# First batch of a fused four-layer block: small operations in another order, trace sums in two banks, weight splits moved

## The chip, the cores and the metric

The kernel runs on one core of a Trainium2 chip. The metric is device time in microseconds (us), the median of several executions. One further execution is taken with the hardware profiler, and the profile's times are counted from the start of its span.

## What is computed

For 16 batches of 256 tokens with 256 features, four residual layers follow each other. The first two, cut to what matters here:

```python
# layer 0: gated multi-time-scale traces (16 time constants, d = 0..15)
ctx   = ema(x, tau_ctx)                                   # scan over the tokens
gated = x * sigmoid([x, ctx] @ Wg.T + bg)
mod   = 0.5 + sigmoid(gelu(x @ Wn1.T + bn1) @ Wn2.T + bn2)     # one value per token and d
temporal = sum_d softmax(blend)[d] * ema(gated * mod[d], tau[d])
soma  = gelu(x @ Wsoma.T + bsoma)
out   = (soma * sigmoid(temporal @ Wtemp.T + btemp)) @ Wout.T
x = x + layernorm(out) * gamma + beta
# layer 1: masked softmax pooling
s = tanh(x @ W1 + b1) @ v
x = x + (softmax(mask(s)) @ x) / count
# layer 2: 8 experts + 1 shared, silu(x@Wg)*(x@Wu)@Wd, mixed by gates
# layer 3: gelu(x@W1+b1)@W2, and an expert part chosen per batch
```

Layers 2 and 3 hold nearly all of the arithmetic.

## The kernel before

**Number format.** Large products run in fp32r as three products of high and low parts. A "split" of an operand is two instructions: the high part is a rounding copy on ScalarE (`rnd("a", ...)`, line 88), the low part is operand minus high part (`low`, line 95), on VectorE (`"v"`) or GpSimd (`"g"`). `mm3` (lines 101 to 103) issues the three products. The first batch's own layers 0 and 1 use plain fp32 products on unsplit operands, so they wait for no split; all later batches need split small weights. These lie side by side in `wh` and `wl`: N1 (256 columns), G (1024, in two halves of 512), SO, TE, OU (512 each), W1 (256). Their unsplit forms are in `small_a` (N1, G, SO, W1) and `small_b` (TE, OU), filled by loads issued by SyncE's queue at the start.

**Stages.** Batch 0 goes through `first_traces` and `first_pooled` by itself. Only then can the expert loop of layer 2 start (first on batch 0 alone, for five of nine experts). Layers 0 and 1 of the later batches (`traces`, `pooled`) are cut into steps by `yield` and dealt out between the units of the expert loop. Batch 1's `traces` begins inside batch 0's `first_pooled`: of the 13 steps after the first 13, steps 16, 20 and 24 are batch 1's (x_1 and its ctx; c, ph, hg, hs; pm, md), and the other ten are batch 0's: 14 pt and tanh, 15 the product with soma, 17 po, statistics and rs, 18 the normalized x1, 19 transposes and x1T, 21 pa and tanh, 22 and 23 the softmax, 25 transposes and q, 26 pp, the addition into acc and the split of it.

**The first batch's traces.** After ph, hg and the gate products pg, `md` gives `mod`'s small rows, and `ms` is their split form. For each d a pair of selecting products spreads two rows over the partitions (`pb`), ScalarE scales them to `mod` (two pieces, line 529, two buffers), GpSimd (VectorE for d=0) multiplies by the gate (`bt`, line 532), VectorE scans (`tr`, two scans, line 535) and TensorE adds the scans up through an identity product (`tacc`, line 538, one 128x512 product in one PSUM bank). At d=5 the soma products and their two Gelus follow (lines 543 to 547). At the end `tacc` is evicted in two halves, one on ScalarE, one on VectorE (`evict`, lines 470 to 475), and pt reads the result.

**Order.** The framework gives each engine a fixed order. It takes it from a timing model: of the instructions that are ready there, the one that stands first in the program. `tc.issue_after(i)` puts the instructions traced inside the block behind `i` on `i`'s engine, and does nothing on other engines. `last_of` holds the latest of some kinds: `"ca"` a rounding copy or eviction on ScalarE, `"cv"` a low part or eviction on VectorE, `"a"` a mod piece, `"g"` a bt, `"tr"` a scan. A split with no such block may be put as early as its operand is there.

**Expert weights.** `load_chunk` loads one chunk (384 KB) into one of two `raw` buffers and splits it into one of ten ring buffers. `prefetch(2, 0)` brings chunks 0 and 1 (low parts on GpSimd) behind the traces; chunks 2 to 5 (low parts on VectorE) are asked for one by one at steps 19, 21, 23 and 25, and four more after step 26.

Of the kernel before, what the change touches and what calls it, by code (L numbers as in the profile page):

```python
# [17 lines left out]
S = 256  # L18
P = 128
# [25 lines left out]
def fused_kernel(  # L45
# [90 lines left out]
    def split_small(c0, n, e):  # L136
        rnd("a", wh[:, c0 : c0 + n], small(c0, n))
        low(e, wl[:, c0 : c0 + n], small(c0, n), wh[:, c0 : c0 + n])
# [117 lines left out]
    held = {}  # L256

    rest = {1: (O_SO, 512), 6: (O_TE, 512), 9: (O_OU, 512), 12: (O_W1, 256)}

    def traces(b):  # L260

        xr = xin_tiles.pop(b)
        xh, xl = hl(f"x_{b}", "hA")
        rnd("a", xh, xr)
        low("g", xl, xr, xh)
# [53 lines left out]
        for d in range(ND):  # L319
            if d % 2 == 0:  # L320
                mod = l0.tile([P, 2, S], F32, tag="mod", name=f"mod{b}_{d}", bufs=2)
                nc.sync.dma_start(mod, mdd[0, d : d + 2].partition_broadcast(P))
            bt = ft("bt", f"bt{b}_{d}", 3)
            tr = tacc if d == 0 else ft("tr", f"tr{b}_{d}", 3)
            with tc.issue_after(last_of[0].ins) if b == 1 and "h" not in last_of else nullcontext():
                for c in range(2):
                    V.scalar_tensor_tensor(
                        bt[:, c], ga[:, c], bl[:, c, d : d + 1], mod[:, d % 2], ALU.mult, ALU.mult
                    )
            for c in range(2):  # L330
                V.tensor_tensor_scan(  # L331
                    tr[:, c], decay[:, d : d + 1].to_broadcast([P, S]), bt[:, c], 0.0, ALU.mult, ALU.add
                )
            if d:
                G.tensor_tensor(tacc, tacc, tr, ALU.add)  # L335
            if b == 1 and d in rest:
                split_small(*rest[d], "g")
            if d == 5:
                soma()
            yield  # L340
# [136 lines left out]
    def first_traces():  # L477
# [14 lines left out]
        def gates_of(ks):  # L492
            for m in range(2):
                for k in ks:
                    i = xr[:, k] if k < 2 else cx[:, k - 2]
                    PE.matmul(pg[m], small(O_G + k * S + m * P, P), i, start=k == 0, stop=k == 3)

        gates_of((0, 1))
        yield
        pm = ps_l.tile([P, 512], F32, tag="ps", name="pm0")  # L500
        last_of["pm"] = PE.matmul(pm[:48, :S], vec[0:64, V_WN2 : V_WN2 + 48], hg[0:64], start=True, stop=True)
        md = l0.tile([48, S], F32, tag="md", name="md0")
        A.activation(md, pm[:48, :S], AF.Tanh, bias=hb[:48, V_BN2 : V_BN2 + 1], scale=0.5)
# [6 lines left out]
        with tc.issue_after(last_of["pm"].ins):  # L510
            gates_of((2, 3))
# [7 lines left out]
        tacc = ps_y.tile([P, 2, S], F32, tag="y0", name="ta0")  # L519
        for d in range(ND):  # L520
# [17 lines left out]
            PE.matmul(tacc, ident, tr, start=d == 0, stop=d == ND - 1)  # L538
            if d == 5:
# [6 lines left out]
                for m in range(2):  # L546
                    A.activation(sm[:, m], pso[:, m], AF.Gelu, bias=vec[:, V_BSO + m : V_BSO + m + 1])
# [3 lines left out]
        for c in range(2):  # L551
            evict(c, t[:, c], tacc[:, c])
# [6 lines left out]
    def first_pooled():  # L559
# [28 lines left out]
        G.tensor_tensor(rs, rs, mhalf, ALU.pow)  # L588
# [354 lines left out]
    while n_steps[0] < FIRST:  # L943
        next(steps)
        if n_steps[0] == 4:
            with tc.issue_after(last_of["cx"].ins):
                later_constants()
    with tc.issue_after(last_of["a"].ins), tc.issue_after(last_of["g"].ins), tc.issue_after(last_of["tr"].ins):
        for off, n in ((O_N1, 256), (O_G, 512), (O_G + 512, 512)):
            split_small(off, n, "g")  # L950
# [4 lines left out]
    while n_done[0] < 1:  # L955
        with tc.issue_after(last_of["ca"].ins), tc.issue_after(last_of["cv"].ins):
            next(steps)
            if n_steps[0] > FIRST + 5 and n < 6 and n_steps[0] % 2:
                prefetch(1, 0)
                n += 1  # L960
    with tc.issue_after(last_of["ca"].ins), tc.issue_after(last_of["cv"].ins):
# [157 lines left out]
```

## Time and profile before

| | |
|---|---|
| median of 3 runs | 2829.91 us (2829.66 to 2830.13) |
| profiled execution, time | 2829.02 us |
| profiled execution, span | 2827.0 us |
| granted TensorE clock, mean over the span | 0.996 |
| TensorE busy | 2774.3 us (98%) |
| VectorE, ScalarE, GpSimd busy | 1454.9, 1248.6, 1299.3 us |
| first expert product | at 60.40 us |

The span goes from the first to the last instruction; some 2 us of the time lie outside it. In lines in order of time the columns are start, duration (or, with a count, from the first's start to the last's end), engine, line of the program, operation, output and inputs by name, shape, count, and in brackets the idle time before it and what ended it. PEld is the weight load of TensorE, which overlaps its products.

### The profile page before, as it was taken

The numbers are of one execution on the slowest core, as the hardware profiler recorded it, in microseconds if no ns is written. First come the engines' busy times: TensorE is split into PE (matmuls) and PEld (weight loads), VectorE is DVE, ScalarE is ACT, GpSimd is POOL, SyncE is SP. The second block draws the span as 40 slices with busy tenths as digits, with TensorE's granted clock in tenths as the row PEclk, the third lists the DMA queues.
The fourth block names the chain that finished last, engine by engine and source line by source line (L and its number), as shares of the span: only waits on it lengthen the run. The fifth ranks groups of instructions, "written<-read, shape, count | busy, mean of one in ns | idle before, by whom it ended". The sixth has DMA issues, their size and how long they took to land.

```text
span 2827.0 us, 36929 instructions
## 1 busy us (share of the span) xinstructions
PE 2774.3 (98%) x13604; PEld 2331.4 (82%) x13604; DVE 1454.9 (51%) x2662; ACT 1248.6 (44%) x2062; POOL 1299.3 (46%) x986
## 2 busy tenths in 40 slices
PE   7889999999999999999999999999999999999999
PEld 4877898888888888888888888888888888888888
DVE  6988877865666363544545444444444542222222
ACT  5565565465444533435334443344433453233334
POOL 5755645544545353544534444444444443333333
PEclk9999999999999999999999999999999999999999
DMA  4453376396443533324433153331533242222453
GB/s 118 138 153 118 104 242 214 121 309 207 151 150 123 177 114 105 120 81 135 153 107 106 41 179 112 108 120 62 177 101 112 92 162 98 90 90 89 167 177 118
DMA packets 116998, 377.53 MB, mean 134 GB/s; under 512 B 12898, under 2 KB 31186, under 8 KB 116818
## 3 DMA queue, kind: packets, MB, share of 16 engines
q1 hardware_dynamic: 116386, 375.11, 40.1%
q8 instruction: 108, 1.77, 0.3%
q14 instruction: 72, 0.59, 0.1%
q10 hardware_dynamic: 432, 0.06, 0.0%
HBM read 310.91 MB, written 64.21 MB: 133 GB/s over the span
## 4 chain that ended last, share of the span: by engine, by line
PE 82%; DVE 7%; DMA 4%; ACT 3%; issue 2%; POOL 1%; SPq 0%; DVEq 0%; ACTq 0%; POOLq 0%
PE pg L102 8%; PE pg L103 8%; PE pg L101 8%; PE pu L103 8%; PE pu L102 8%; PE pu L101 8%; PE y L103 8%; PE y L102 8%; PE y L101 8%; DMA raw_e<-in_wexp_dram 4%; DVE w_e L95 2%; DVE tr L331 1%; ACT w_e L88 1%; PE z L101 1%; PE z L103 1%
## 5 line engine op out<-in xcount | busy, mean ns | idle before, releaser
L95 POOL TENSOR_TENSOR hh<-h,hh 128x512 fp32r<-128x512 f32 x640 | 847.7, 1325 | 1318.8 <-ACT hh L88 1298.2
L743 DVE TENSOR_TENSOR h<-h,pu 128x512 f32<-128x512 f32 x576 | 393.9, 684 | 907.4 <-PE pu L103 805.6
L88 ACT ACTIVATE hh<-h 128x512 fp32r<-128x512 f32 x640 | 403.5, 631 | 933.8 <-DVE h L743 911.6
L101 PE MATMUL pg<-x,w_e 128*128 128x512 f32 (+1 forms) x1232 | 466.0, 378 | 10.2 <-DVE h L743 6.4
L742 ACT ACTIVATE h<-pg 128x512 f32<-128x512 f32 x576 | 343.1, 596 | 299.1 <-PE pg L103 236.5
L101 PE MATMUL pu<-x,w_e 128*128 128x512 f32 (+1 forms) x1232 | 465.3, 378 | 6.9 <-ACT h L742 6.7
L103 PE MATMUL pg<-x,w_e 128*128 128x512 f32 (+1 forms) x1232 | 464.6, 377 | 1.5 <-DVE w_e L95 1.2
L102 PE MATMUL pg<-x,w_e 128*128 128x512 f32 (+1 forms) x1232 | 464.4, 377 | 1.1 <-POOL x L95 1.1
L102 PE MATMUL y<-hh,w_e 128*128 128x512 f32 (+1 forms) x1232 | 462.8, 376 | 2.2 <-POOL hh L95 2.2
L102 PE MATMUL pu<-x,w_e 128*128 128x512 f32 (+1 forms) x1232 | 463.5, 376 | 0.0
L103 PE MATMUL pu<-x,w_e 128*128 128x512 f32 (+1 forms) x1232 | 463.4, 376 | 0.0
L103 PE MATMUL y<-hh,w_e 128*128 128x512 f32 (+1 forms) x1232 | 462.7, 376 | 0.0
L101 PE MATMUL y<-hh,w_e 128*128 128x512 f32 (+1 forms) x1232 | 416.2, 377 | 2.8 <-ACT hh L88 1.6
L335 POOL TENSOR_TENSOR ta<-ta,tr 128x512 f32<-128x512 f32 x225 | 310.5, 1380 | 87.3 <-DVE tr L331 77.1
L331 DVE TENSOR_TENSOR_SCAN tr<-decay,bt 128x256 f32<-128x256 f32 x450 | 285.6, 671 | 0.0
L101 PEld LDWEIGHTS pg<-x,w_e 128*128 128x128 f32 x1232 | 232.3, 189 | 54.1 <-DVE h L743 8.9
L101 PEld LDWEIGHTS pu<-x,w_e 128*128 128x128 f32 x1232 | 232.5, 189 | 50.4 <-ACT h L742 9.5
L101 PEld LDWEIGHTS y<-hh,w_e 128*128 128x128 f32 x1232 | 231.5, 189 | 46.8 <-ACT hh L88 2.6
L102 PEld LDWEIGHTS y<-hh,w_e 128*128 128x128 f32 x1232 | 232.4, 189 | 44.6 <-POOL hh L95 2.9
L103 PEld LDWEIGHTS pg<-x,w_e 128*128 128x128 f32 x1232 | 232.4, 189 | 44.4 <-DVE w_e L95 2.0
L103 PEld LDWEIGHTS pu<-x,w_e 128*128 128x128 f32 x1232 | 232.5, 189 | 41.9
L103 PEld LDWEIGHTS y<-hh,w_e 128*128 128x128 f32 x1232 | 232.3, 189 | 41.8
(279 smaller groups left out, 3263.2 us busy)
## 6 DMA issues: line engine op xcount, KB each, us to landing
w_e<-keep_e SPq DMA_DIRECT2D x216, 768.0 KB, 4.2
raw_e<-in_wexp_dram SPq DMA_DIRECT2D x160, 384.0 KB, 3.7
keep_e<-w_e SPq DMA_DIRECT2D x72, 768.0 KB, 4.3
mod<-mdd SPq DMA_DIRECT2D x120, 256.0 KB, 3.6
w_f<-keep_f SPq DMA_DIRECT2D x56, 384.0 KB, 3.5
raw_c<-in_comb_dram SPq DMA_DIRECT2D x32, 260.0 KB, 2.7
xr<-in_xT_dram SPq DMA_DIRECT2D x16, 256.0 KB, 3.5
xt<-in_x_dram SPq DMA_DIRECT2D x16, 256.0 KB, 2.6
```

Source lines behind the costliest of these rows:

```text
L88: last_of["ca"] = A.activation(out_, in_, AF.Copy)
L95: i = (V if e == "v" else G).tensor_tensor(out_, in_, h.bitcast(F32), ALU.subtract)
L101: PE.matmul(o, wh, xh, start=start, stop=False, **kw)
L102: PE.matmul(o, wh, xl, start=False, stop=False, **kw)
L103: last_of["pe"] = PE.matmul(o, wl, xh, start=False, stop=stop, **kw)
L331: V.tensor_tensor_scan(tr[:, c], decay[:, d : d + 1].to_broadcast([P, S]), bt[:, c], 0.0, ALU.mult, ALU.add)
L335: G.tensor_tensor(tacc, tacc, tr, ALU.add)
L742: A.activation(h, ps_g, AF.Silu)
L743: last_of["h"] = V.tensor_tensor(h, h, ps_u, ALU.mult)
```

## The change

The soma Gelus move from d=5 to d=9 and d=11, each behind the latest mod piece. The gate products are issued as: first half (x part), pm behind it, second half (x part), then both ctx parts. The trace sum is kept in two banks, one per half, with two 256-wide products per d. Batch 1's x is split right behind the traces instead of in step 16. The splits of SO, TE, OU and W1, which stood in batch 1's trace loop, are taken apart: high parts behind md; low parts on VectorE, TE in step 21, the others in step 25. The high parts of N1 and G stay behind the traces, as does N1's low part; G's low parts go to GpSimd behind rs (step 17). The prefetch of steps 19 to 25 now stands in a block of its own that is entered after the step, so it is put behind the `ca` and `cv` of that step instead of those before it.

```diff
--- before.py
+++ after.py
@@ -133,8 +133,10 @@
     def load_small(c0, c1):
         nc.sync.dma_start(small(c0, c1 - c0), wsmall[:, c0:c1])
 
-    def split_small(c0, n, e):
-        rnd("a", wh[:, c0 : c0 + n], small(c0, n))
+    def high_small(c0, n):
+        A.activation(wh[:, c0 : c0 + n], small(c0, n), AF.Copy)
+
+    def low_small(c0, n, e):
         low(e, wl[:, c0 : c0 + n], small(c0, n), wh[:, c0 : c0 + n])
 
 
@@ -254,15 +256,20 @@
         return l0.tile([P, 2, S], F32, tag=tag, name=name, bufs=bufs)
 
     held = {}
-
-    rest = {1: (O_SO, 512), 6: (O_TE, 512), 9: (O_OU, 512), 12: (O_W1, 256)}
+    early_x = {}
+
+    def split_x(b):
+        xh, xl = hl(f"x_{b}", "hA")
+        rnd("a", xh, xin_tiles[b])
+        low("g", xl, xin_tiles[b], xh)
+        early_x[b] = xh, xl
 
     def traces(b):
 
+        if b not in early_x:
+            split_x(b)
+        xh, xl = early_x.pop(b)
         xr = xin_tiles.pop(b)
-        xh, xl = hl(f"x_{b}", "hA")
-        rnd("a", xh, xr)
-        low("g", xl, xr, xh)
         cx = ft("ta", f"ctx{b}")
         for c in range(2):
             V.tensor_tensor_scan(
@@ -333,8 +340,6 @@
                 )
             if d:
                 G.tensor_tensor(tacc, tacc, tr, ALU.add)
-            if b == 1 and d in rest:
-                split_small(*rest[d], "g")
             if d == 5:
                 soma()
             yield
@@ -489,18 +494,18 @@
         A.activation(hg, ph[:, :S], AF.Gelu, bias=vec[:, V_BN1 : V_BN1 + 1])
         pg = two("pg0")
 
-        def gates_of(ks):
-            for m in range(2):
-                for k in ks:
-                    i = xr[:, k] if k < 2 else cx[:, k - 2]
-                    PE.matmul(pg[m], small(O_G + k * S + m * P, P), i, start=k == 0, stop=k == 3)
-
-        gates_of((0, 1))
+        def gates_of(m, ks):
+            for k in ks:
+                i = xr[:, k] if k < 2 else cx[:, k - 2]
+                last_of["pg"] = PE.matmul(pg[m], small(O_G + k * S + m * P, P), i, start=k == 0, stop=k == 3)
+
+        gates_of(0, (0, 1))
         yield
         pm = ps_l.tile([P, 512], F32, tag="ps", name="pm0")
-        last_of["pm"] = PE.matmul(pm[:48, :S], vec[0:64, V_WN2 : V_WN2 + 48], hg[0:64], start=True, stop=True)
+        with tc.issue_after(last_of["pg"].ins):
+            last_of["pm"] = PE.matmul(pm[:48, :S], vec[0:64, V_WN2 : V_WN2 + 48], hg[0:64], start=True, stop=True)
         md = l0.tile([48, S], F32, tag="md", name="md0")
-        A.activation(md, pm[:48, :S], AF.Tanh, bias=hb[:48, V_BN2 : V_BN2 + 1], scale=0.5)
+        last_of["md"] = A.activation(md, pm[:48, :S], AF.Tanh, bias=hb[:48, V_BN2 : V_BN2 + 1], scale=0.5)
         V.tensor_scalar(md, md, 0.5, 1.0, ALU.mult, ALU.add)
         ms = l0.tile([48, S], F32R, tag="ths", name="ms0")
         rnd("v", ms, md)
@@ -508,7 +513,9 @@
         yield
         ga = ft("ga", "ga0")
         with tc.issue_after(last_of["pm"].ins):
-            gates_of((2, 3))
+            gates_of(1, (0, 1))
+            for m in range(2):
+                gates_of(m, (2, 3))
         for m in range(2):
             A.activation(ga[:, m], pg[m], AF.Tanh, bias=hb[:, V_BG + m : V_BG + m + 1], scale=0.5)
         for c in range(2):
@@ -516,7 +523,7 @@
         yield
         sm = ps_a.tile([P, 2, S], F32, tag="ga", name="sm0")
 
-        tacc = ps_y.tile([P, 2, S], F32, tag="y0", name="ta0")
+        tacc = [ps_y.tile([P, 512], F32, tag=f"y{c}", name=f"ta0{c}")[:, :S] for c in range(2)]
         for d in range(ND):
             if d % 2 == 0:
                 pb = ps_gu.tile([P, 2, S], F32, tag="gu", name=f"pb0_{d}")
@@ -535,7 +542,8 @@
                 last_of["tr"] = V.tensor_tensor_scan(
                     tr[:, c], decay[:, d : d + 1].to_broadcast([P, S]), bt[:, c], 0.0, ALU.mult, ALU.add
                 )
-            PE.matmul(tacc, ident, tr, start=d == 0, stop=d == ND - 1)
+            for c in range(2):
+                PE.matmul(tacc[c], ident, tr[:, c], start=d == 0, stop=d == ND - 1)
             if d == 5:
                 pso = ps_l.tile([P, 2, S], F32, tag="ps", name="pso0")
                 with tc.issue_after(last_of["pb"].ins):
@@ -543,13 +551,15 @@
                         for k in range(2):
                             w = small(O_SO + k * S + m * P, P)
                             PE.matmul(pso[:, m], w, xr[:, k], start=k == 0, stop=k == 1)
-                for m in range(2):
+            if d in (9, 11):
+                m = (d - 9) // 2
+                with tc.issue_after(last_of["a"].ins):
                     A.activation(sm[:, m], pso[:, m], AF.Gelu, bias=vec[:, V_BSO + m : V_BSO + m + 1])
             if d % 2:
                 yield
         t = ft("bt", "t0", 3)
         for c in range(2):
-            evict(c, t[:, c], tacc[:, c])
+            evict(c, t[:, c], tacc[c])
         xt = xt_tiles.pop(0)
         with tc.issue_after(last_of["g"].ins):
             last_of["g"] = G.tensor_tensor(xt, xt, bet.unsqueeze(1).to_broadcast([P, 2, S]), ALU.add)
@@ -585,7 +595,7 @@
             V.bn_stats(st[:, t], po[t])
             V.bn_aggr(mv[:, t], st[:, t])
         V.tensor_scalar(rs, mv[:, :, 1], 4e-5, None, ALU.add)
-        G.tensor_tensor(rs, rs, mhalf, ALU.pow)
+        last_of["rs"] = G.tensor_tensor(rs, rs, mhalf, ALU.pow)
         for t in range(2):
             V.scalar_tensor_tensor(po[t], po[t], mv[:, t, 0:1], gam, ALU.subtract, ALU.mult)
         yield
@@ -945,9 +955,18 @@
         if n_steps[0] == 4:
             with tc.issue_after(last_of["cx"].ins):
                 later_constants()
+
+
+    gates_w = ((O_G, 512), (O_G + 512, 512))
+    rest_w = ((O_SO, 512), (O_OU, 512), (O_W1, 256))
+    with tc.issue_after(last_of["md"].ins):
+        for off, n in ((O_TE, 512), *rest_w):
+            high_small(off, n)
     with tc.issue_after(last_of["a"].ins), tc.issue_after(last_of["g"].ins), tc.issue_after(last_of["tr"].ins):
-        for off, n in ((O_N1, 256), (O_G, 512), (O_G + 512, 512)):
-            split_small(off, n, "g")
+        split_x(1)
+        for off, n in ((O_N1, 256), *gates_w):
+            high_small(off, n)
+        low_small(O_N1, 256, "g")
         prefetch(2, 0)
 
 
@@ -955,9 +974,17 @@
     while n_done[0] < 1:
         with tc.issue_after(last_of["ca"].ins), tc.issue_after(last_of["cv"].ins):
             next(steps)
+        pool = last_of.get("rs", last_of["g"])
+        with tc.issue_after(last_of["ca"].ins), tc.issue_after(last_of["cv"].ins), tc.issue_after(pool.ins):
+            if n_steps[0] == 17:
+                for off, k in gates_w:
+                    low_small(off, k, "g")
             if n_steps[0] > FIRST + 5 and n < 6 and n_steps[0] % 2:
                 prefetch(1, 0)
                 n += 1
+
+            for off, k in {21: ((O_TE, 512),), 25: rest_w}.get(n_steps[0], ()):
+                low_small(off, k, "v")
     with tc.issue_after(last_of["ca"].ins), tc.issue_after(last_of["cv"].ins):
         coefs()
         prefetch(RING - n)
```

## The prediction

> **What bounds the kernel now.** I read the stretches of the run first, then the chain that ended last, then each engine's instructions in order of time for the first 62 us, because all that the change touches runs there.
>
> TensorE is busy 98% of the span. What it loses it loses at the front: busy time falls short by some 15 us before 60 us, and by some 27 us between 60 and 400 us, where the stretches show VectorE full and TensorE waiting for it.
>
> ```profile
> PE 2774.3 (98%) x13604; PEld 2331.4 (82%) x13604; DVE 1454.9 (51%) x2662; ACT 1248.6 (44%) x2062; POOL 1299.3 (46%) x986
> 90.00:100.00 10.00, 7.74 (x59) 7.06 (x58) 10.00 (x18) 2.80 (x4) 8.45 (x6) 1.00 0.42 131
> 300.00:400.00 100.00, 98.06 (x645) 88.70 (x644) 80.96 (x136) 61.92 (x105) 48.48 (x34) 1.00 0.50 160
> ```
>
> (In the stretches: length, then busy us of PE, PEld, DVE, ACT, POOL, granted clock.) The first expert matmul starts at 60.40. Until then the first batch is one chain, and all that starts behind it starts with it. So the question is by how much 60.40 moves, and whether the rest moves along.
>
> The chain's first part, by instructions in order of time:
>
> ```profile
> 11.74 0.42 ACT L88 ACTIVATE wh<-small_a 128x256 fp32r<-128x256 f32 x1 [0.81 <-DMA small_a<-in_wsmall_dram]
> 12.07 0.45 ACT L503 ACTIVATE md<-pm,hb 48x256 f32<-48x256 f32 x1
> 13.21 0.69 DVE L90 CAST ms<-md 48x256 fp32r<-48x256 f32 x1
> 14.94 2.50 ACT L529 ACTIVATE mod<-pb,bl 128x256 f32<-128x256 f32 x6 [1.70 <-PE pb L524]
> 20.53 15.98 POOL L532 TENSOR_TENSOR bt<-ga,mod 128x512 f32<-128x512 f32 x13 [1.46 <-ACT mod L529]
> 21.82 15.99 DVE L535 TENSOR_TENSOR_SCAN tr<-decay,bt 128x256 f32<-128x256 f32 x26 [1.45 <-POOL bt L532]
> 39.03 0.38 ACT L473 ACTIVATE t<-ta 128x256 f32<-128x256 f32 x1 [1.30 <-PE ta L538]
> 39.45 0.42 DVE L475 COPY t<-ta 128x256 f32<-128x256 f32 x1 [1.63 <-ACT t L473]
> ```
>
> See four things. A split of a later batch's weight, waiting for its load, stands ahead of md in ScalarE's queue. The trace loop then runs at 15.98/13 = 1.23 us per trace on GpSimd and as much (two scans) on VectorE. It stopped once, for 1.46, while mod stood behind the soma Gelu (18.76, ScalarE idle 1.33 for pso). At the end VectorE's eviction waits for ScalarE's, out of the same bank.
>
> The second part, near 48 us:
>
> ```profile
> 47.27 0.95 DVE L95 TENSOR_TENSOR w_e<-raw_e,w_e 128x768 fp32r<-128x768 f32 x1
> 48.53 0.36 ACT L473 ACTIVATE x1T<-ptr0g 128x256 f32<-128x256 f32 x1
> 49.30 0.42 DVE L475 COPY x1T<-ptr0u 128x256 f32<-128x256 f32 x1
> 59.47 0.42 DVE L645 TENSOR_TENSOR acc<-x1T,pp0g 128x256 f32<-128x256 f32 x1 [1.90 <-PE pp0g L643]
> 62.66 2.11 DVE L95 TENSOR_TENSOR w_e<-raw_e,w_e 128x768 fp32r<-128x768 f32 x1 [0.41 <-ACT w_e L88]
> ```
>
> The transposes end at 47.84, but ScalarE and VectorE take x1T only after a chunk's split and batch 1's c, hg, hs.
>
> **The change, part by part.** Times are those of the old trace; a gain moves all behind it.
>
> *Start.* The high parts of TE, SO, OU, W1 go behind md, their low parts leave GpSimd at 9 to 14 us, and pm is issued between the two halves of the gates. pm: 10.17 to 9.21 (end of the first gate pair); md: 12.07 to 9.75, done 10.2. VectorE's constants and md, ms ran stretched beside those GpSimd subtractions (the kind_i cast took 1.28, ms 0.69); without them ms is there at about 11.2 instead of 14.35. But ga does not come earlier: the same gate matmuls and pm still end at 12.73, the second tanh at 13.24. From there four mod pieces of 0.42 end at 14.92, and GpSimd's first bt starts at 14.95 instead of 16.59: **1.65**. What is late next is the gates. The four highs cost ScalarE 3x0.55+0.35 = 2.0 between md (10.2) and the first tanh (11.8, not the last): 0.4 over, hidden by the second tanh. If the order puts all of them behind the tanh, the loop starts 2.0 later and this part is -0.35; if pb slips in front of the gates it is 1.9. I take 1.65, as all four operands were there by 11.74.
>
> *Soma Gelu to traces 9 and 11.* The 1.46 goes. ScalarE has 0.39 free per trace (0.84 of 1.23); a Gelu of 0.46 exceeds it by 0.07, twice: **+1.3**. The last scan moves from 37.81 to 34.86. VectorE does not forbid it: 32 scans of 0.615 from 14.8 end at 34.5.
>
> *Two banks.* Two 256-wide products replace a 512-wide one of about 1.05 us; each pt product of 256 took about 0.43, so the loop's TensorE time is unchanged (sixteen more loads of ident hide beside it; if not, 0.2 a trace at most, under the 1.23). From the last scan to the last pt it took 41.46-37.81 = 3.65: sum, eviction, eviction, four pt. With c=0 summed and evicted during the last scan: 0.55 for the c=1 sum, 0.45 to evict, 1.0 for the last two pt, in all 2.05: a gain of 1.6. Against it, ScalarE's queue after the last mod (32.0) now holds x_1, N1, the two gates and two chunks, 3.6, so until 35.6, and the c=0 sum is there at 34.9: between 0 and 0.7 lost; I take 0.3. **+1.3**. Running sum 4.25.
>
> *GpSimd after the loop.* xt, x_1, N1, two chunks: 1.27+1.25+0.65+3.6 = 6.8 from 33.6 is 40.4; rs comes at 45.65-4.25 = 41.4. Before, it came 0.02 after GpSimd got free. Cost nothing, with 1 us of cover. The gates' low parts follow rs; their first reader is batch 1's gate product after 62 us.
>
> *Chunks of the prefetch.* In the old loop the waits of step and prefetch are taken together; in the new one the prefetch takes them after the step, so chunk 2 and then c, hg, hs stand behind x1T. x1T at 47.85 lets the second pa go 1.1 earlier. But the tanh th now has chunk 2, c, hg, hs ahead of it on ScalarE: 0.83+0.55+0.46+0.35 = 2.2 from 48.1, so 50.3 instead of 51.02. Chunk 3 (0.75) falls between th and the table load of 1.28: Exp at 52.8 instead of 53.27. No transfer is late by it: chunk 2's buffer is freed by GpSimd's chunk 0, which comes 4 us sooner; chunk 5's low part ends near 58 instead of 57.04, so chunk 7's load (about 3.1) lands at 61.1, before ScalarE takes it (61.9 now).
>
> *Low parts on VectorE.* TE (0.69 by the row of c at 48.13) lies in a wait of 2.09 at 50.7. SO, OU, W1 (0.69+0.69+0.42) come before the acc addition; with md 0.28 and chunk 5's 0.95 they are 3.03 from 56.4, so 59.45, and acc stood at 59.47. That eats the 0.5 won just before. Both parts together: **+0.2**, between -1.0 and +1.1. Here a rule speaks against the change. Chunk 2's low part took 0.95 with GpSimd idle, 2.11 at 62.66 with GpSimd on a chunk. The Trainium skill, "GPSIMD Engine Reference", 1. Specifications, says the two engines share SBUF interfaces and contend when a VectorE instruction has two SBUF inputs; each new low part has two. By the rule alone the four double, 2.5 more, and the gain would be 2.0. By the rows GpSimd is idle from 46.43 to 61.97 but for 1.59 at 50.24; the gates' low parts fill 2.5 us after rs, beside chunk 2 and c, not beside SO, OU, W1. TE may double, inside its 2.09. I go by the rows and keep the 2.5 for the range.
>
> *Behind 60 us.* Nothing is removed there: the splits written into batch 1's trace loop already ran at 8 to 14 us. VectorE's queue is the same and starts earlier, so the 27 us of waits shift whole. 0, between -2 and +2.
>
> Sum: 1.65+1.3+1.3+0.2 = 4.45. The profiled execution took 2829.02 for a span of 2827.0 (2.0 outside); the span becomes 2822.55, that time 2824.6. The median of the runs is 0.9 above the profiled one: 2829.91-4.45 = 2825.5.
>
> **Rivals.** 0.2% is 5.66 us, about what a measurement of this kernel can tell from no change.
>
> *A, the sum holds:* 2825.5, itself between 2823 and 2828. Chance 0.48; a third of that passes the bound at 2824.25.
>
> *B, the clock comes back too.* The second half of the chain runs cold:
>
> ```profile
> 46.00:48.00 2.00, 1.37 (x9) 0.74 (x7) 1.58 (x4) 1.97 (x5) 0.44 (x1) 1.00 0.45 172
> 58.00:60.00 2.00, 2.00 (x6) 1.29 (x4) 0.42 (x1) 0.07 (x1) 0.00 (x0) 0.50 0.86 329
> ```
>
> (the clock is the third figure from the end). The clock halves after TensorE was busy 0.48 of 2 us at 44. The Trainium skill, "TensorE: Matmul & The Clock Gate", Part 1, has a free-running window of about 3.4 us, whose load sets it. The gap before pa shrinks by 0.8, so the fall may come later. At full clock the chain's pa 0.6, psc 0.6, ppt 0.3 and three pp (0.86 to 0.43 each) 1.3 would give 2.8 more: 2822.7. For: the shorter gap. Against: ph of batch 1 leaves that gap, and pa to pp wait often. With other waits that may vanish, 0.27.
>
> *C, given back later.* The chain turns to DMA and VectorE at 64 us, and TensorE waits at 186 for batch 1's split. If that point is held by transfers instead of the chain, 60.40 moves and it does not: 2829.5. Against: its queue is VectorE's, 95% full. 0.13.
>
> *D, slower: low parts in front of acc.* Steps' low parts stand ahead of acc in VectorE's queue. Stretched as at 62.66 (2.2 times), 2.5 become 5.5; the gap is 1.9, so acc slips 3.6 and the gain falls to 0.85. The chunks' low parts behind slip as much, and each frees one of only two raw buffers: two rounds of 3.6 are 7.2 us of supply. Net 6.4 slower: 2836.3. It decides if the first expert matmul comes after 60.4. Against: GpSimd has nothing queued there. 0.12.
>
> **Numbers.** Faster by over 0.2%: 0.16 of A and B's 0.27, 0.43. Within: 0.32 of A and C, 0.45. Slower: 0.12. The likeliest is A. The range, 2821 to 2831.5, holds A, C and most of B, and leaves out D and B's far end.
>
> **What would show it.** In the new profile: bt's first on GpSimd near 15.0 and no stop of 1.4; the last scan near 34.9; VectorE's t not behind ScalarE's; pt over by 37.2; x1T straight after the transposes; SO, OU, W1 over before acc; first expert matmul near 56. A last scan after 36.5 makes the start wrong; 56 with an unmoved end is C; low parts of over 1 us ahead of acc are D; clock 1.0 from pa to pp is B.

## The result, and the profile after

| | before | after |
|---|---|---|
| median | 2829.59 us (22 runs) | 2833.6 us (22 runs, 2829.35 to 2839.56) |
| profiled execution, time; span | 2829.02; 2827.0 us | 2829.35; 2827.5 us |
| first expert product | 60.40 us | 56.92 us |

The ratio is 1.0014 [1.0009, 1.002]: slower by 4.0 us, where 4.45 less were forecast, and outside the range. The profiled execution is the fastest of the 22, so its trace shows less loss than the median has. Its front looks much as forecast. The chain's first part, instructions in order of time of the kernel after:

```profile
9.88 0.47 ACT L508 ACTIVATE md<-pm,hb 48x256 f32<-48x256 f32 x1 [1.42 <-PE pm L506]
10.70 0.29 DVE L90 CAST ms<-md 48x256 fp32r<-48x256 f32 x1
13.09 2.50 ACT L536 ACTIVATE mod<-pb,bl 128x256 f32<-128x256 f32 x6
14.74 18.48 POOL L539 TENSOR_TENSOR bt<-ga,mod 128x512 f32<-128x512 f32 x15 [13.35 <-ACT mod L536]
14.69 19.84 DVE L542 TENSOR_TENSOR_SCAN tr<-decay,bt 128x256 f32<-128x256 f32 x32
34.85 0.38 ACT L478 ACTIVATE t<-ta 128x256 f32<-128x256 f32 x1
35.31 0.42 DVE L480 COPY t<-ta 128x256 f32<-128x256 f32 x1 [0.79 <-PE ta L546]
```

md no longer stands behind a waiting split; GpSimd's 15 bt run in one piece from 14.74 (forecast 14.95); the last scan ends at 34.53 (forecast 34.86); VectorE's t waits for its own sum and not for ScalarE. The second part, with SyncE's queue and ScalarE behind it:

```profile
43.18 0.38 ACT L478 ACTIVATE x1T<-ptr0g 128x256 f32<-128x256 f32 x1 [5.40 <-PE ptr0g L611]
43.40 0.42 DVE L480 COPY x1T<-ptr0u 128x256 f32<-128x256 f32 x1 [0.69 <-PE ptr0u L611]
54.82 0.95 DVE L95 TENSOR_TENSOR w_e<-raw_e,w_e 128x768 fp32r<-128x768 f32 x1
55.99 0.42 DVE L655 TENSOR_TENSOR acc<-x1T,pp0g 128x256 f32<-128x256 f32 x1 [0.23 <-PE pp0g L653]
56.92 0.39 PE L101 MATMUL pg<-x,w_e 128*128 128x256 f32 x1 [0.17 <-ACT x L88]
56.22 0.80 SPq L329 DMA_DIRECT2D mod<-mdd  x2
57.13 6.79 SPq L682 DMA_DIRECT2D raw_e<-in_wexp_dram  x3
61.72 0.85 ACT L88 ACTIVATE w_e<-raw_e 128x768 fp32r<-128x768 f32 x1 [3.32 <-DMA raw_e<-in_wexp_dram]
```

x1T follows its transposes at once (but pa, which reads it, does not start at once: see below); the acc addition waits for its product and not for the low parts ahead of it; the first expert product is 3.48 earlier. But ScalarE now waits 3.32 for a chunk (chunk 7) that stands ahead of the table load for the first Silu. That Silu starts at 63.88, where it was 63.94. A new wait at the handover takes most of the front's gain, at first. The page's row for the engines and the four stretches shown of before:

```profile
PE 2775.1 (98%) x13636; PEld 2335.3 (83%) x13636; DVE 1455.0 (51%) x2666; ACT 1249.5 (44%) x2062; POOL 1294.1 (46%) x982
46.00:48.00 2.00, 1.44 (x5) 0.62 (x3) 1.97 (x2) 0.65 (x2) 1.02 (x1) 0.50 0.64 197
58.00:60.00 2.00, 2.00 (x19) 2.00 (x19) 0.68 (x4) 0.40 (x1) 1.52 (x1) 1.00 0.99 263
90.00:100.00 10.00, 7.86 (x52) 7.49 (x51) 10.00 (x20) 3.33 (x5) 7.39 (x6) 0.83 0.50 144
300.00:400.00 100.00, 97.94 (x648) 88.79 (x647) 81.38 (x136) 60.86 (x103) 47.37 (x34) 1.00 0.51 162
```

The clock still falls before pa (0.50 at 46). It is at 1.00 from 58 on, where expert products run now. TensorE has 32 more products and 32 more loads than before (13604 each). That pair of numbers turned out to matter most.

To see where the rest goes I matched the h addition (VectorE's `h<-h,pu`, one for each unit of the expert loop, numbered from 0) between two traces and took the difference. The lag against the first profile of before, in us, with the columns' names those of the runs below:

```
unit (at)      after  after_again  before_again  before_aa
1    (71)      -2.14     +0.40        -1.13        -0.46
31   (247)     -1.11     +2.76        -1.15        -0.19
84   (500)     -1.09     +3.75        -0.63        -0.91
88   (518)     -0.41     +4.23        -0.63        -0.91
94   (545)     -0.41     +4.23        -0.63        -0.91
100  (599)     +1.23     +5.17        -0.39        -0.93
end            +0.5      +5.9         -0.5         -0.9
```

Three losses: at the start (after_again, whose profiled execution is the slowest of its 13, never had the gain), between the first product and the second h, and in two steps at 500 to 518 and at 545 to 599, hundreds of microseconds behind anything that was edited.

### The profile page after: what moved, and what is told of

Its sections match the earlier page's. It is cut to its first block, busy times and chain, and to the rows that moved or that the text cites. A ratio compares the mean times of both kernels' runs of the same rounds, so it can differ in the third digit from the quotient of the medians.

```text
span 2827.5 us, 36992 instructions
## 1 busy us (share of the span) xinstructions
PE 2775.1 (98%) x13636; PEld 2335.3 (83%) x13636; DVE 1455.0 (51%) x2666; ACT 1249.5 (44%) x2062; POOL 1294.1 (46%) x982
## 3 DMA queue, kind: packets, MB, share of 16 engines
q8 instruction: 108, 1.77, 0.3%
## 4 chain that ended last, share of the span: by engine, by line
PE 82%; DVE 6%; DMA 5%; ACT 3%; issue 2%; POOL 1%; SPq 0%; DVEq 0%; ACTq 0%; POOLq 0%
PE pg L102 8%; PE pg L103 8%; PE pg L101 8%; PE pu L103 8%; PE pu L102 8%; PE pu L101 8%; PE y L101 8%; PE y L103 8%; PE y L102 8%; DMA raw_e<-in_wexp_dram 4%; DVE w_e L95 2%; ACT w_e L88 1%; DVE tr L338 1%; PE z L101 1%; PE z L102 1%
## 5 line engine op out<-in xcount | busy, mean ns | idle before, releaser
L101 PEld LDWEIGHTS pu<-x,w_e 128*128 128x128 f32 x1232 | 232.2, 189 | 51.5 <-ACT h L752 10.7
```

Source lines behind the costliest of these rows:

```text
L101: PE.matmul(o, wh, xh, start=start, stop=False, **kw)
```

## The experiments

Medians are of this kernel and of before on the same chip, each with its ratio and interval; 12 to 22 runs of a changed kernel, 22 to 65 of before. "Order" is each engine's fixed order.

### The handover at 60 us: SyncE's queue, and the prefetch's block

Three kernels on one chip: after unchanged; after with chunk 7's load ahead of batch 1's mod transfers (which wait for mdd); after with the prefetch back in the step's own block.

```diff
 # after_sp
+    with tc.issue_after(last_of["raw", 0, 7].ins) if b == 1 and d == 0 else nullcontext():
         nc.sync.dma_start(mod, mdd[0, d : d + 2].partition_broadcast(P))
...
-            nc.sync.dma_start(raw, wexp[key[2]])
+            last_of["raw", key[1], key[2]] = nc.sync.dma_start(raw, wexp[key[2]])
 # after_pf
         with tc.issue_after(last_of["ca"].ins), tc.issue_after(last_of["cv"].ins):
             next(steps)
+            if n_steps[0] > FIRST + 5 and n < 6 and n_steps[0] % 2:
+                prefetch(1, 0)
+                n += 1
```

> The changed kernel itself, timed and profiled once more. Its first profile has the first expert product 3.5 us earlier, a gain of 2.1 left from the second product of the loop on, and 0.5 us lost at the end, but its median is 4 us above before, so one trace doesn't show where most of the loss lies. Theory 1 (the loss is made at the transfers, between 230 and 800 us, and differs from run to run): front as in the first trace within 0.2 us, the lag to before then moves by several us between 400 and 800 us, at other places than in the first trace. Theory 2 (a fixed cost of the new order right behind the front): the same lag curve as in the first trace within 0.3 us, and the time near 2829.5. Ratio to before 1.001 to 1.002 by both.

> The changed kernel with one edit: batch 1's mod transfers are put behind chunk 7's load on SyncE's queue, as they stood before; the order of every engine is otherwise the same. In the changed kernel chunk 7's load goes out at 57.1 behind two mod transfers that wait for mdd, and ScalarE's first Silu stands behind chunk 7's high part. Theory 1a (this queue order eats 1.3 of the front's 3.5 us, and nothing more): first h 3.3 to 3.6 us earlier than before instead of 2.1, the median 1.3 below the changed kernel's. Theory 1b (the late chunk also sets the loss in the transfers behind it): median 4 to 6 us below the changed kernel's, at 2826 to 2828. Rival (the front's gain is lost at a later point whatever it was): lag at 500 us as in the changed kernel, median the same within 1 us.

> The changed kernel with one part undone: chunks 2 to 5 are prefetched inside the step's own block again, so their splits are put behind the step before, as before the change. Theory 1: chunk 7's load is in front of the mod transfers again, so the first h gains the 1.3; x1T waits for chunk 2 again (0.7 to 1.1 lost): lag at the first h about -2.5, and the median 1 us or less from the changed kernel's. Theory 3 (the new place of the prefetch is what spoils the transfers of the loop): median 4 us or more below the changed kernel's.

Measured: after_again 2831.95 against 2828.47, 1.0011 [1.0002, 1.0019]; after_sp 2832.55, 1.0012 [1.0006, 1.0019]; after_pf 2835.05, 1.0022 [1.0016, 1.0029]. In after_sp the first h came 2.38 earlier than in before's first profile, the second only 1.21, and the median did not move: the queue's order makes the first stall but is not the cause of the result. after_pf reorders the loop on several engines as well, so it tells only that this undoing does not help; its median is 3.1 above after_again's, where the one theory had at most 1 between them and the other 4 or more below.

### Was the first profile of before typical?

> The kernel before, profiled once more, as the measure of how far two traces of one kernel differ. Theory 1: also here the lag between the two traces moves between 400 and 800 us, by under 1.5 us, and is under 0.3 us up to 230 us. Theory 2: the two traces lie within 0.3 us throughout.

before_again is one more profiled execution of the unchanged kernel (2828.53); before_aa, below, another. Neither theory came: the two traces are 1.1 apart from the second h on (see the table above).

```profile
15.36 1.99 PE L545 MATMUL pso<-xr,small_a 128*128 128x256 f32 x8
16.64 18.52 POOL L532 TENSOR_TENSOR bt<-ga,mod 128x512 f32<-128x512 f32 x15 [2.83 <-ACT mod L529]
```

These two lines, PE's and GpSimd's of before_again, have no counterpart in the first profile. There pso took 3.43 for the same eight products, and GpSimd stopped 1.46 for it. Here pso takes 1.99, and the 15 bt run in one piece, as in the traces of the padded kernels below; only before_aa lost something there (its bt took 19.34 from first to last). What differed is TensorE's granted clock while pso ran. Stretches of before and before_again (third figure from the end):

```profile
16.00:18.00 2.00, 2.00 (x6) 1.64 (x5) 1.89 (x4) 1.35 (x4) 1.42 (x2) 0.50 0.89 352
16.00:18.00 2.00, 1.78 (x9) 1.16 (x8) 1.90 (x4) 1.88 (x6) 1.36 (x2) 1.00 0.98 391
```

before_aa has 0.52 there; the other five traces with before's front have 1.00. The first expert product is at 59.07 (59.72 in before_aa), not 60.40.

### Instructions alone: idle products added to before

The two banks add 16 products; in plain fp32 each is two instructions and two weight loads, together 64 instructions on TensorE. Its instructions come by transfer: the page's row for that queue is

```profile
q8 instruction: 108, 1.77, 0.3%
```

108 packets of 1.77/108 = 16.4 KB for 2x13604 = 27208 products and loads: one for every 256 or so (27208/256 = 106; with TensorE's waiting instructions the trace has 27643, and 27643/256 = 108). The traces with 256 or more added have 109. The Trainium skill, "Trainium Architecture — The Big Picture", The software stack, says that instructions are 64 bytes, and 16 KB over 64 is 256: the page and the trace agree. Sixty-four instructions more ahead of a given point bring every later fetch a quarter of a block forward. Start times of fetches by the transfer records of that queue (not a row of the page):

```
before         218.6  250.3  391.3  403.8  510.9  565.1  589.9
after          207.6  241.3  381.0  396.7  505.4  551.6  580.0
before_pe320   209.7  243.5  382.9  398.9  508.4  553.2  581.6
after_pad256   218.3  249.9  390.1  402.7  510.5  564.0  588.6
```

So I put one-element products on the identity into idle time of TensorE, ahead of ph, where it waits for weights. Nothing reads them.

```diff
     make_identity(nc, ident)
+    pad = ps_a.tile([P, 2, S], F32, tag="ga", name="pad")
+    for _ in range(16):     # before_pe64; 32: before_pe128; 64: before_pe256
+        PE.matmul(pad[0:1, 0, 0:1], ident[:, 0:1], ident[:, 0:1], start=True, stop=True)
```

The names give the number of added instructions. before_pe64 and before_pe128 keep before's order; before_pe256 swaps two weight splits on ScalarE and two loads on SyncE in the first 10 us.

> The kernel before with 16 one-element fp32 products added on TensorE in its idle time ahead of ph (64 TensorE instructions with their weight loads, as many as the two-bank sums add); the order of every engine is otherwise the same. In the traces the instruction fetches of TensorE (16 KB each, some every 15 to 30 us, on the same DMA engines as the chunk loads) fall at 218.6 and 250.3 before, at 207.6 and 241.3 after the change, and chunk loads 58, 96 and 115 land later in all traces of the changed kernel (3.7 to 4.2-5.7, 5.9 to 6.3-7.2, 3.8 to 5.1-6.2 us from issue to split). Theory F (more TensorE instructions move the fetches into transfers that bind; that is what eats the gain): fetches at the changed kernel's places, those chunks late as there, median 2 to 5 us above before, as the changed kernel itself though nothing of its order is here. Rival S (the loss comes from the changed order and its earlier front): median within 1 us of before, chunks as before. A front later by the added products would show as a constant lag from the first product on.

> As the kernel with 64 added TensorE instructions, with 256 (64 one-element products), one whole 16 KB block if an instruction takes 64 bytes: the fetches return to the old places in the program. Theory F: whatever the front is late by, nothing is lost behind it: the lag at the end is the lag at the first expert product within 1 us. Rival F2 (it is the number of instructions, not the place of the fetches): lost four times what 64 lose. Rival S: lag at the end is the lag at the first expert product.

> The kernel before with 128 added TensorE instructions: half a block, so the fetches fall at third places. Theory F: chunks are late at other places than with 64, and the median differs from both 0 and 64 added, by -2 to +6 us; no sign can be told. Rival F2: 3 to 5 us above before, as with 64 and 256. Rival S: as before within 1 us.

> The kernel before with 256 added TensorE instructions once more, since its first time (3.6 above before, interval 0.05 to 0.21%) stood against its trace (fetches and chunks as before). Theory F: within 1.5 us of before. Rival F2 (added instructions cost whatever their number): 3 to 5 us above before again.

> The kernel before against itself: the measure for the other three. All theories: ratio 1.0000 within its interval; a third trace of its front, in which the soma products take 3.4 us with the clock at half or 2.0 with it at full, and the stop of 1.46 in the trace loop comes with the first alone.

Measured against 2828.05 to 2828.2: before_pe64 2832.85, 1.0016 [1.0009, 1.0023]; before_pe128 2831.36, 1.0011 [1.0004, 1.0017]; before_pe256 2831.62, 1.0013 [1.0005, 1.0021], repeated 2829.78, 1.0006 [0.9997, 1.0014]; before_aa 2828.08, 0.9999 [0.9991, 1.0007]. Sixteen idle products in an idle moment, and nothing else, make before slower by as much as the whole change did. before_pe256 does not fit as well: by the fetch theory its lag at the end had to be that at the first product within 1 (it went from -0.7 to +1.1), and its repetition had to be within 1.5 of before (1.6). Rival F2, that added instructions cost 3 to 5 whatever their number, fits before_pe64 (4.8), before_pe128 (3.2) and the first before_pe256 (3.6), not its repetition; after_pad256, below, stands against it.

The last experiment of this kind parts the place of the fetches from the number of instructions: before_pe256 with 16 products more behind po, so that fetches fall as in before_pe64, a block later.

> before_pe256 (before with 64 one-element products ahead of ph) and 16 such products more behind po: 320 TensorE instructions more than before, so that the fetches fall as in before_pe64 (one block later). All else in the order of before_pe256. Fetch theory: as before_pe64, +3 to +5 us, units 84 to 88 and 94 to 100 lose about 0.7 each. Count theory (each added instruction costs the same wherever it stands): 1.25 times before_pe256, so +2 to +4.5, without the steps at 84 and 94. Neither: within 1.5 of before.

Measured: 2834.44, 1.0021 [1.0013, 1.003]. Lags at units 84, 88, 94, 100: before_pe256 0.53, 0.52, 0.52, 0.71; before_pe320 0.96, 1.87, 1.87, 3.69. The steps of after are back. Over all twenty traces, units 84 to 100 lose 1.4 to 2.7 in six (after, after_again, after_sp, after_pf, before_pe64, before_pe320), and between -0.4 and 0.4 in the other fourteen. Where TensorE waited between 540 and 600 us, by the view of waits (what waited, for whom: us in total, times, longest). In before:

```profile
PE z L101 <- DVE acc L790: 2.1, 1, 2.1
PE z L101 <- ACT hh L88: 1.1, 1, 1.1
```

In after:

```profile
PE z L101 <- DVE acc L800: 2.1, 1, 2.1
PE z L101 <- ACT hh L88: 1.6, 1, 1.6
PE pg L101 <- DVE h L753: 0.9, 1, 0.9
```

In before_pe320:

```profile
PE z L101 <- DVE acc L796: 2.1, 1, 2.1
PE pg L101 <- DVE h L749: 1.8, 1, 1.8
PE z L101 <- ACT hh L88: 1.0, 1, 1.0
```

The wait of pg for h is new in both. What is behind it stands on ScalarE, in order of time, a little earlier. In before:

```profile
582.41 0.85 ACT L88 ACTIVATE w_e<-raw_e 128x768 fp32r<-128x768 f32 x1 [1.22 <-DMA raw_e<-in_wexp_dram]
```

In after:

```profile
583.77 0.85 ACT L88 ACTIVATE w_e<-raw_e 128x768 fp32r<-128x768 f32 x1 [2.49 <-DMA raw_e<-in_wexp_dram]
```

In before_pe320:

```profile
586.29 0.84 ACT L88 ACTIVATE w_e<-raw_e 128x768 fp32r<-128x768 f32 x1 [3.33 <-DMA raw_e<-in_wexp_dram]
```

The load of this chunk, from its issue to its split, took 3.81 in before, 5.09 in after, 5.93 in before_pe320. In the last two an instruction fetch starts while it runs (580.0 and 581.6); in before the nearest are at 565.1 and 589.9. Over all twenty traces this load took 4.82 to 6.15 in the six in which one of TensorE's fetches falls in it (the six with the steps), and 3.81 to 4.60 in the other fourteen. ScalarE's split waits longer, the Silu comes later, and TensorE stops for h.

### Fetches put back in the kernel after

192 instructions more in after (32 products ahead of ph, 16 behind po) make one whole block with the two banks' 64; the order stays after's.

```diff
     make_identity(nc, ident)
+    pad = ...        # as above, range(32)
...
+        pad2 = ps_a.tile([P, 2, S], F32, tag="ga", name="pad2")
+        for _ in range(16):
+            PE.matmul(pad2[0:1, 0, 0:1], ident[:, 0:1], ident[:, 0:1], start=True, stop=True)
         x1 = ft("x1", "x10")
```

> The changed kernel with 192 one-element TensorE instructions added (32 products ahead of ph, 16 behind po, some 26 ns each), which with the 64 of the two banks make one 16 KB block; the order of every engine is otherwise that of the changed kernel. Theory F: fetches fall where they fell before the change (near 250, 404 and 590 instead of 241, 397 and 580), nothing is lost at 500 to 520 and 545 to 600, and the median is 3 us or more below the changed kernel's, at 2826 to 2829. Rival S (front and queue order, not the fetches): median within 1.5 us of the changed kernel's, 4 us above before.

> The kernel after with 192 added TensorE instructions (32 one-element products ahead of ph, 16 behind po), a repetition of after_pad256, whose ratio was 1.0002. Fetch theory (where TensorE's instruction fetches fall is what makes after slower): 0.5 to 1 us around before, ratio 0.9995 to 1.0007, h units 84 to 88 and 94 to 100 lose less than 0.3 each. Chance theory (the first time was a lucky one): ratio about 1.0013, as after.

Measured: 2829.26, 1.0002 [0.9994, 1.0011]; repeated 2828.36, 1.0003 [0.9994, 1.0011]. Units 84 to 100 lose 0.1 and 0.2 in all. Adding work took some 3 us off the kernel after (by the ratios: 1.0014 and 1.0011 without it). Both agree with the fetch theory, and the repetition speaks against a lucky run. Rival F2 fails here: 256 instructions more than before, and no loss clear of noise.

Two other ways to put the fetches back also changed the loop's order (the timing model takes another path): the sum in one bank again (`tacc` one tile, one product of 512), and all 48 products ahead of ph.

> The changed kernel with the trace sums in one bank again (one 512-wide product per trace): TensorE has as many instructions as before. The front loses the 1.3 to 1.6 us of the two banks. Theory F: the fetches stand where they stood before, chunks 58, 96 and 115 land as before, and the median is 3 us or more below the changed kernel's, at 2826 to 2829. Rival S: 1.3 us above the changed kernel's.

> The changed kernel with 192 TensorE instructions added ahead of ph (48 one-element products): with the 64 of the two banks one whole block, so the fetches return to the places of before, if the front is not late by it. Theory F: lag at the end equal to the lag at the first expert product within 1.5 us. Rival S: 3 us or more lost between 230 and 700 us as in the changed kernel.

Measured: 2833.05, 1.0016 [1.0009, 1.0023], and 2832.52, 1.0014 [1.0007, 1.002]. Units 84 to 100 lost nothing in either (-0.4 and -0.2). But their lags grew to 6.72 and 5.13 by unit 20 (192 us), where the order is theirs alone. They confirm the steps. The fetch theory's forecasts for both as a whole failed (a median at 2826 to 2829; a lag at the end within 1.5 of that at the first product); with the loop's order changed as well, they do not decide between it and the rival.

### What is left of the front's gain

On the padded kernel: after_sp's edit (best_sp, twice), and besides the low parts of SO, OU, W1 behind chunk 5's (best_low).

```diff
 # best_low, besides after_sp's edit
+            with tc.issue_after(last_of["cv"].ins):
                 for off, k in {21: ((O_TE, 512),), 25: rest_w}.get(n_steps[0], ()):
                     low_small(off, k, "v")
```

> after_pad256, and batch 1's first two mod transfers stand behind chunk 7's load on SyncE's queue; all else in the same order. If the queue's order is what loses the front's gain: h0 near 62.3 and h1 at least 1.5 earlier than in after_pad256, and that 1.5 is kept: ratio about 0.9997. If chunk 5's late low part is what does it (it holds the raw buffer of chunk 7): h1 within 0.5 of after_pad256 and the same median.

> best_sp, and the low parts of SO, OU and W1 stand behind chunk 5's low part on VectorE, instead of ahead of it (TE's likewise behind its chunk's). Theory chunk 5: its low part ends near 54.6 instead of 55.8, chunk 7's load starts 1.2 earlier, first product about 0.3 later at most (acc behind 1.8 of low parts), h1 1.2 earlier than best_sp; the gain of the front reaches h1: ratio about 0.9993, 2826 us. Rival: the supply of chunks 6 to 9 is held by the transfers themselves, h1 moves less than 0.4, ratio as best_sp.

Measured: best_sp 2827.55, 0.9999 [0.9991, 1.0007]; best_low 2829.47, 1.0004 [0.9996, 1.0012]. Chunk 5's low part now ends at 58.24 in best_low and 58.95 in best_sp, the acc addition starts 0.5 later, and the second h comes at the same time (within 0.06). The 1.2 us expected from that order did not come. best_sp's own expectation, a second h at least 1.5 ahead of after_pad256's (68.92), failed too: it came at 70.73, because the first product was late.

Why was best_sp's first product at 60.11 and after's at 56.92? TensorE's products during the gates, in order of time. In after:

```profile
9.77 1.13 PE L500 MATMUL pg0u<-xr,small_a 128*128 128x256 f32 x4
11.60 1.03 PE L500 MATMUL pg0u<-ctx,small_a 128*128 128x256 f32 x4
```

In after_again:

```profile
10.58 2.07 PE L500 MATMUL pg0u<-xr,small_a 128*128 128x256 f32 x4
12.45 1.91 PE L500 MATMUL pg0g<-ctx,small_a 128*128 128x256 f32 x4
14.15 1.27 PE L500 MATMUL pg0u<-ctx,small_a 128*128 128x256 f32 x4
```

In best_pm (below):

```profile
9.50 1.14 PE L503 MATMUL pg0u<-xr,small_a 128*128 128x256 f32 x4
```

Four instructions take about 1.9 until a certain moment and about 1.0 after it. In after that moment is before 9.8, in after_again at 14.5. In nine traces with pm behind both halves' x parts (before's eight and best_pm) it lay between 8.7 and 11.4. In eleven traces with pm between the halves it lay between 8.6 and 10.7 five times and between 14.2 and 15.1 six times. best_pm puts pm back there in best_sp:

```diff
         gates_of(0, (0, 1))
+        gates_of(1, (0, 1))
         yield
...
-            gates_of(1, (0, 1))
```

> best_sp with pm behind both halves of the gates' x parts, as in before; all else in the same order on every engine but SyncE, where one load of x changes places. If pm between the halves holds TensorE's fast clock back: the products turn fast before 11.8 (not at 14 to 15), VectorE's first bt starts at 14.0 to 15.0, the first expert product at 57 to 58, and the median is 1 to 2 us below best_sp's: ratio to before 0.9993 to 0.9996. If the moment of the fast clock is chance: late with a chance of 6 in 10, and the median within 0.7 of best_sp's.

> best_sp unchanged, as the pair of best_pm. By both theories: median near 2827.6 (ratio 0.9999), and the products turn fast at 8.6 to 10.7 or at 14 to 15.2, by chance.

Measured: best_pm 2827.24 against 2827.15, 1.0001 [0.9992, 1.0009]; best_sp_again 2827.4, 1.0002 [0.9994, 1.001]. best_pm turned fast near 9.5 as expected, VectorE's first bt came at 15.04 (14.05 in best_sp_again, 17.17 in best_sp), but the median did not fall by 1 to 2. That half of the expectation failed. best_sp_again spread over 10 us (2823.18 to 2833.16), best_pm over 4 (2825.29 to 2829.09), but best_sp's first runs over 4 too. So pm's place goes with the late moment in the traces (none of nine, six of eleven), and what that costs the median is not settled. No version here beats before.

## Why the prediction was wrong

From -4.45 to +4.0 it is 8.45 us. Two misses make up most of it: some 3 for a cost that was set at nothing, and some 3.9 of a gain of which 0.5 is left at the second h on average. About 1.5 is not accounted for.

**A cost was set at nothing.** The step *Two banks* has "sixteen more loads of ident hide beside it": it counted their time on TensorE and not that TensorE's instruction stream grew by 64. That is the step that decided the sign. Sorted by what the added instructions leave over whole blocks of 256 (the ratio less 1, in units of 0.0001):

```
left over 64, before:           before_pe64 16   before_pe320 21
left over 64, after:            after 14   after_again 11   after_sp 12
left over 128:                  before_pe128 11
left over 0, before:            before_aa -1   before_pe256 13, 6
left over 0, after:             after_pad256 2, 3   best_sp -1, 2   best_low 4   best_pm 1
the loop in another order:      after_pf 22 (64 over)   after_onebank 16, after_pe192 14 (0 over)
```

Where the loop keeps its order, the kernels after fall from about 12 to 2 when the remainder goes: 0.0010, some 3 us of the 4.0. before_pe320 against before_pe256 (21 against 13 and 6) is the same move the other way. What stays open is why before_pe256 is not at 0, and before_pe128 not either, whose profiled execution shows +0.5 only. For before_pe256 the traces show a part: in both of its executions TensorE's granted clock is 0.50 from 186 to 190 us, with 512-wide products of 0.63 instead of 0.39, where before's is 1.00, and the lag grows by 1.07 and 1.08 between units 19 and 20. Whether the added instructions bring that about is not shown; best_pm, with the same 0.50, loses 1.07 there too, while traces with a fall of half that length there lose nothing between these units.

**The gain was sized on one execution.** *Soma Gelu* (+1.3) removed a stop that of eight traces with before's front only the first has in full (1.46; before_aa about 0.8); with pso at 1.99 there is nothing to remove. That it stood in the one trace that was read is bad luck. *Start* (+1.65) holds in the traces that turn fast early (bt on GpSimd at 14.7 to 15.7 against 16.4 to 17.4 in before's) and is negative in the others (17.5 to 18.0). Before was not so exposed: bt came at 16.59 where TensorE turned fast near 9 and md stood behind the waiting split, and at 16.64 in before_again, where it turned at 11.4 and md waited for pm (1.14) and for no split. Of *Two banks*' 1.3, 0.9 is there: from the last scan to the last pt 37.27-34.53 = 2.74 against 3.65. The first product stands at 59.6 on average over seven traces of before's front (before, again, aa, pe64, pe256 twice, pe320) and at 58.4 over seven of after's (after, again, sp, pad256 twice, best_sp twice): a gain of 1.2, not 4.45.

**A wait was left out of *Chunks of the prefetch*.** The prediction had "x1T at 47.85 lets the second pa go 1.1 earlier". pa went later, counted from the transposes. In before and in after:

```profile
48.95 2.03 PE L608 MATMUL pa<-x1T,small_a 128*128 128x256 f32 x4 [1.10 <-ACT x1T L473]
45.24 2.08 PE L618 MATMUL pa<-x1T,small_a 128*128 128x256 f32 x4 [1.88 <-ACT hg L288]
```

x1T is there at 43.8 in after. But pa takes the one PSUM buffer of the tag `ps` in `ps_l` that batch 1's ph holds until ScalarE's hg has read it, and hg now stands behind x1T, chunk 2's high part and c (44.72 to 45.19). From the first transpose to pa it is 2.77 in after and 1.94 in before. From the last pt to the first product it is 19.65 against 18.94: this part with *Low parts on VectorE*, forecast at +0.2, measured -0.7. It is no accident of one trace: pa waits 1.87 to 1.98 for hg in all of after's that keep the prefetch's new block.

**Of the gain at the first product, part does not reach the second h.** The prediction had "chunk 7's load (about 3.1) lands at 61.1, before ScalarE takes it (61.9 now)". ScalarE came 3.5 earlier with the rest and waited for it 3.32; mod's transfers, waiting for mdd, had slipped ahead of it on SyncE's queue. From the first product to the second h it took 10.43 in before, 11.77 in after. At the second h the same fourteen traces are 0.5 apart on average.

**Behind 60 us, "waits shift whole"** failed as well: the loads there are sensitive to what else uses the DMA engines, and the fetches moved.

**The rivals.** B did not come: pa took 2.08 for four instructions at half clock. D neither: SO, OU and W1's low parts took 0.67, 0.68 and 0.41, unstretched, with GpSimd idle from 47.01 to 58.48 as the rows had it, and acc waited for its product. C is nearest in shape (60.40 moved, the end did not), but for another reason and with another sign. None held the cost of the added instructions, and the range left the result out.

## What to carry to other kernels

Count an edit's instructions, not only their time: on an engine with tens of thousands of them the stream itself is fetched by transfers, and a few more shift every later fetch, here into a load that binds. Test it by adding idle instructions to the old kernel: if they do what the change does, the change's own merit has not been measured yet. Take a second profile of before ahead of costing a stall: one that stands in a single execution is not there to be gained. And ask of every instruction that is to go earlier not only when its operands are there but who holds the buffer that it writes.

## What the hardware showed that was not expected

- Sixteen one-element products, 0.94 us in a wait, cost 4.8 us (2832.85 against 2828.05); 48 of them made another kernel faster (1.0002 and 1.0003 of before, after 1.0011 to 1.0014).
- An instruction fetch of 16 KB takes 1.1 us on average by its records, at most 2.7, and a 384 KB load that it met took 4.82 to 6.15, without one 3.81 to 4.60. In after the fetch took 1.87 and the load 1.28 more than in before; in after_sp 0.88 and 2.34. Why it can be more than the fetch itself is not shown.
- The time at which TensorE turns fast moved from 8.6 to 15.1 us between executions. The Trainium skill, "TensorE: Matmul & The Clock Gate", Part 1, has the transition some 4 us into sustained work, 0.5 either way, with a free-running window of 3.4. The products began at 5.9; the early traces lie about that, but wider (2.7 to 5.5 behind); the late ones (8.3 to 9.2) do not, though TensorE was busy the whole time but for pauses of about 0.1 around pm. The measurement decides: here it can come some 4 us later. The profile's granted clock doesn't tell it. Stretches of after_again and after (third figure from the end):

```profile
10.00:12.00 2.00, 2.00 (x5) 1.17 (x4) 0.74 (x3) 1.31 (x3) 0.00 (x0) 1.00 0.72 78
10.00:12.00 2.00, 2.00 (x10) 1.77 (x10) 0.99 (x3) 2.00 (x5) 0.00 (x0) 1.00 0.85 141
```

Both say 1.00, with 5 products in the one and 10 in the other. So the product's own duration is what to read; that it is the clock is an inference.
